# Two cross-attention layers: the beginning in a written order on all engines, loads queued behind the stacks, and a scale moved to ScalarE

## The chip, the cores and the metric

The kernel runs on one core of a Trainium2 chip. A core has a matrix engine (TensorE, PE in the profile), three engines for elementwise work (VectorE or DVE, ScalarE or ACT, GpSimd or POOL), a queue that does nothing here but issue transfers (SyncE or SP), and DMA engines that carry the transfers between the chip's memory and the on-chip buffers. Each engine works through its own list of instructions in order and waits on semaphores for the others. The metric is the device time of one launch in microseconds. Timed runs vary by a few us, and the profile is one more execution of the same program with the hardware profiler on.

## The reference: two attention layers with image tokens

The inputs are x (16 batches, 256 tokens, 320 channels) and a context of 16 x 256 tokens x 512 channels. Two layers follow one another, each with 20 heads of 16 channels. Cut to what matters, layer 0 is:

```python
text, ip = context[:, :77], context[:, 77:]          # 77 text tokens, 179 image tokens
q, k_text, v_text = x @ Wq, text @ Wk, text @ Wv
text_out = softmax(heads(q) @ heads(k_text).T / 4) @ heads(v_text)
scores = heads(q) @ heads(ip @ Wk_ip).T / 4
text_probs = softmax(q @ k_text.T / 4)               # over all 320 channels, no heads
sem = (text_probs @ text) @ ip.T / 4                 # the semantic term
ip_probs = softmax(scores + 0.5 * sem) * spatial_mask
out = (text_out + ip_probs @ heads(ip @ Wv_ip)) @ Wout + bout + x
```

Layer 1 takes that output as its x, with 252 text and 4 image tokens, and a semantic term for each head from normalised vectors. The change touches layer 0 only, in its beginning and in its repeated part.

## The kernel before

**Numbers.** Products with weights and context are made in a reduced float format (fp32r). Each operand is split into a high part and a low part: `halves` (L148 to L153) copies the high part on ScalarE (L150) and subtracts it from the source on VectorE or GpSimd (L153). A product is then three matmuls: high by high, high by low, low by high (`prod`, L238; `prod_m`, L248 for the third m-tile).

**Slots.** In layer 0 the 20 heads go in five groups of four, so 16 batches make 80 slots, each of one batch and one group. Slots 80 to 159 are layer 1. A slot of layer 0 has these steps:

- `stacks0` loads the slot's K and Q "stacks" by SP: 48 rows of keys or queries from the DRAM tiles kd and qd, which hold them as hi, hi, lo, and 77 rows that carry the semantic term (qs<-tph on the Q side, ks<-M on the K side). Two more rows carry the maxima and two constant "fields" that say to which token each maximum belongs. There are four stacks in a ring, and they are loaded four slots ahead (`LEAD`).
- `score0` multiplies them (PE, tile S, L728), and VectorE takes the maxima of text and image scores (L729, L730).
- `maxima0` turns the maxima on PE (L736), copies them on ScalarE (L738) and writes them into the Q stack with four small DMAs, issued by ScalarE (L740), or by SP for the first two slots.
- `turned0` makes the transposed scores with the maxima already subtracted (PE, tile T, L752), takes the exponential on ScalarE (L755), and GpSimd multiplies it by rs, the exponential of the semantic term (L758).
- `attend0` and `settle0` multiply by the values and normalise (L785, L796 to L803).

**Tasks.** Everything that is done per batch or per pair of batches is a task with due times in slots: keys (`keys0`, a pair at a time, with the context load and its split), queries (`queries0`: the x load, its split into hq at L583 to L585, three products at L595 and L598, the qd writes), semantic scores (`semantic0`), tokens, values, closing. The call `fill(now)` runs each task's next piece when its time has come. The order on PE is therefore written by hand everywhere.

**The other engines.** After the beginning, the order on SP, ScalarE, VectorE and GpSimd is chosen when the program is built, by a scheduler that simulates time. Only where `queued` is called, an instruction is kept behind the last one that was marked by `anchor` on its engine. In `begin`, all engines follow the order in which the instructions are written, but what stands before `begin` in the file (the loads and splits of the first weights and the first context in `all_halves`, the memsets, the fields) is placed by the scheduler.

**The beginning.** `keys_first` makes the first pair's keys: three m-tiles of text keys, then three of image keys, each m-tile over four chunks of the context before the next. Then come the first batch's queries, its semantic scores, the second batch's queries, the stacks and the first scores; SP issues all of it in one queue. PSUM, the matrix engine's output memory, is used in banks: two for T, one for P, three for X, and S.

**semantic0.** Of each batch it makes two tiles of 128 queries by 77 text tokens: scores (L651), their sum (L653 on ScalarE, L654), the maximum (L657, L658), the exponential with its sum (L662), the reciprocal (L665) and the scale by it (L666, VectorE), and the transposition on PE (L670) with its copies (L672, L673).

**Semaphores of the DMAs.** In the built program, the DMAs of SP and ScalarE take eight completion semaphores in turn, and each waits until the one before it on the same semaphore has completed. So which DMA a small maxima load waits for depends on how many DMAs lie between.

Of the kernel before, what the change touches and what calls it, by code (L numbers as in the profile page):

```python
# [17 lines left out]
S = 256  # L18
H = 20
# [30 lines left out]
def xattn2(  # L50
# [31 lines left out]
    def dma(out, in_):  # L82
        nc.sync.dma_start(*(f(ap) if ap.dtype == FR else ap for ap in (out, in_)))  # L83
# [5 lines left out]

    def bank(tag="X"):  # L90
        return ps.tile([128, 512], F32, tag=tag, name=tag, bufs=BANKS[tag])
# [35 lines left out]
    nc.scalar.copy(ident_r, ident)  # L127
    tmask = const_tile([128, 7], "tmask")
    dma(tmask, tmask_d)
# [89 lines left out]

    def all_halves(jobs, rings):  # L220

        waiting = []
        for src, hi, lo, tag in jobs:
            while sum(w[3] == tag for w in waiting) == rings[tag]:
                halves(*waiting.pop(0)[:3])
            raw = buf(tag, [128, 512], bufs=rings[tag])
            raw = raw[:, : src.shape[1]] if len(src.shape) == 2 else raw.rearrange("p (k n) -> p k n", k=src.shape[1])
            dma(raw, src)
            waiting.append((hi, lo, raw, tag))
        for w in waiting:  # L230
            halves(*w[:3])
# [30 lines left out]
    def context(b, n, wait=0):  # L262
# [8 lines left out]
        yield from in_turn(parts, wait, "rawc raw" if b == 2 and n == 2 else "rawc", nc.gpsimd if wait and b != 2 else nc.vector)  # L271
        if n == 2:
# [3 lines left out]

    ct = [buf(t, [128, 2, 512], FR, bufs=2, name="ct") for t in ("cta", "cta", "ctb", "ctb")]
    ctx0 = [(cT_d[k * 128 : (k + 1) * 128, : 2 * S], ct[k][:, 0], ct[k][:, 1]) for k in range(4)]
# [6 lines left out]
    RINGS = {"P": SIZES["NP"], "raw": SIZES["RAW"], "rawc": 2}  # L285
    all_halves(
        [job for k in range(4) for job in (
            (*ctx0[k], ("rawc", "raw")[k // 2]), (rows(wk0_d, k), *rounded(wkt[:, k]), "P"))],
        RINGS,
    )  # L290
    x0 = buf("xq", [128, 3, S])
    dma(x0, xT_d[0].rearrange("(k p) t -> p k t", p=128))
    all_halves(
        [(rows(wq0_d, k), *rounded(wqt[:, k]), ("rawc", "raw")[k // 2]) for k in range(3)]
        + [(rows(wki0_d, k), *rounded(w), "P") for k, w in enumerate(wkit)],
        RINGS,
    )
    nc.vector.tensor_scalar_mul(wqt[:, 2, CH : 2 * CH], f(wqt[:, 2, CH : 2 * CH]), tmask[:, 3:4])
    wvt, wvit = buf("wC", [128, 2, 4, 320], FR), [buf("wD", [128, 2, 2, 320], FR, bufs=2) for j in range(2)]
    all_halves(  # L300
        [(rows(wv0_d, k), wvt[:, 0, k], wvt[:, 1, k], ("rawc", "raw")[k % 2]) for k in range(4)]
        + [(rows(wvi0_d, k), wvit[k // 2][:, 0, k % 2], wvit[k // 2][:, 1, k % 2], ("rawc", "raw")[k % 2]) for k in range(4)],
        RINGS,
    )
    wv0, wvi0 = [lambda s, k: wvt[:, s, k]], [lambda s, k: wvit[k // 2][:, s, k % 2]]
    wq, wo = [lambda s, k, m: wqt[:, k, columns(s, m)]], []

# [3 lines left out]
    ind0 = buf("raw", [128, 512], bufs=SIZES["RAW"], name="ind0")[:2, :S]  # L311
    dma(ind0, ind0_d)
    ind0r = buf("mt", [8, S], FR, name="ind0r")[:2]
    nc.scalar.copy(ind0r, ind0)
    for i in range(SIZES["NR"]):
        nc.gpsimd.memset(f(ks[i]), 0.0)
        nc.gpsimd.memset(f(qs[i]), 0.0)
        dma(ks[i][XROW + T0 : KS0], ind0r.unsqueeze(1).to_broadcast([2, 4, S]))
# [3 lines left out]
    for v in vr:  # L322
        nc.gpsimd.memset(v, 0.0)
        for t in range(2):
            nc.vector.tensor_scalar_add(
                vcols(v, V0W)[:, t, :, 16], vcols(v, V0W)[:, t, :, 16], tmask[:, t : t + 1]
            )
        nc.vector.memset(vcols(v, V0W)[:, 2, :, 16], 1.0)
# [3 lines left out]
    nc.vector.memset(zone, 0.0)  # L332
    nc.vector.memset(zone[:, 21:22], 1.0)
    hsn = const_tile([128, 3, 8, 2, 16], "hsn")
    nc.gpsimd.memset(f(buf("q", [128, 2, 3, S], FR))[64:, :, 2], 0.0)
# [37 lines left out]
    def keys_first():  # L373
# [6 lines left out]
        for w, lo, hi, a, z in ((wk0, 0, T0 + 1, 0, T0), (wki0, T0 - 1, S, T0, S)):  # L380
            for m in range(3):
                kp = bank()[:, : 2 * (hi - lo)].rearrange("p (b t) -> p b t", b=2)
                prod_m(kp, w, m, lambda s, k: ct(s, k)[:, :, lo:hi], 4)
                n = 64 if m == 2 else 128
                evacuate(kst[m][:, 0, :, a:z], kst[m][:, 1, :, a:z], kp[:, :, a - lo : z - lo], m)
                if a:
                    keys_out(kd[0][0], m, kst[m], slice(0, 1))
                else:
                    nc.gpsimd.tensor_copy(kt[:n, m, :, :, :T0], f(kst[m][:n, :, :, :T0]))
                yield  # L390
# [188 lines left out]
    def split(src, neg, eng, tag):  # L579

        hl = buf(tag, [128, 5, S], FR)
        order = queued if tag == "hq" else lambda inst: inst
        order(nc.scalar.copy(hl[:, 0:3], src))  # L583
# [711 lines left out]
```

## Time and profile before

| | |
|---|---|
| median of 3 timed runs | 1550.69 us (1549.12 to 1552.69) |
| the profiled execution | 1542.26 us |
| its span | 1540.4 us |
| PE busy | 1441.0 us, 94% |
| VectorE busy | 1207.8 us, 78% |
| GpSimd busy | 1203.6 us, 78% |
| ScalarE busy | 872.8 us, 57% |
| mean granted clock of TensorE | 0.978 |
| HBM read, written | 118.04 MB, 77.10 MB |

The span is what the profile covers; the profiled execution's own time lies 1.86 us above it, and 8.43 us below the median of the timed runs. In rows of the timeline stand the start (us from the span's start), the duration, the engine, the line of the kernel, the operation, the tile written and the tiles read, and in brackets how long the engine was idle before and which engine, tile or line ended that. An engine name with a q (SPq, ACTq) is its sequencer, which issues DMAs. In the views of waits stand the engine and line that waited, what released it, the total in us, the count and the longest. In a table by windows stand, for each stretch, the busy time and count of each engine, TensorE's granted clock as a share of full speed, the DMA engines' busy share and GB/s. A PE row's end is modelled, and matmuls overlap, so PE's share says where it is idle better than how fast it works.

### The profile page before, as it was taken

To read this page: it belongs to the slowest core of one execution; us is meant where nothing else is said; L and a number is where in the kernel's file an instruction comes from. 1 tells how busy PE (TensorE), PEld (TensorE's weight loads), DVE (VectorE), ACT (ScalarE), POOL (GpSimd) and SP (SyncE) were. 2 spreads that over 40 slices of the span, in tenths; PEclk is the share of its full clock that TensorE was granted. 3 is DMA by queue.
4 is the path that set the end of the run, shared out by engine and by line. 5 is a ranking of instruction groups with operands and counts; after the bars stand their busy time and mean duration, and the time that the engine had idled before them with its cause. 6 is when DMAs were issued, how large, how long until landed. Compare 5 with 4: busy or idle time off the path is not lost.

```text
span 1540.4 us, 36105 instructions
## 1 busy us (share of the span) xinstructions
PE 1441.0 (94%) x12726; PEld 1162.6 (75%) x12726; DVE 1207.8 (78%) x2659; ACT 872.8 (57%) x1941; POOL 1203.6 (78%) x1274
## 2 busy tenths in 40 slices
PE   6789999999999989788999999999999999999996
PEld 5678888878787878567777777777777777777764
DVE  6458888777777788867778888888887887788885
ACT  5345555555564545546665666566656666666561
POOL 4258797979797978878587788877987798779785
PEclk9889999999999999989999999999999999999997
DMA  6756777676766666765444344444444344434311
GB/s 208 204 179 175 218 192 215 189 218 188 217 192 201 190 202 172 207 199 153 117 123 117 115 137 110 117 130 120 117 119 136 108 121 124 132 106 113 100 32 36
DMA packets 228815, 233.04 MB, mean 151 GB/s; under 512 B 38410, under 2 KB 198508, under 8 KB 228620
## 3 DMA queue, kind: packets, MB, share of 16 engines
q1 hardware_dynamic: 226428, 229.44, 52.5%
q8 instruction: 102, 1.67, 0.5%
q10 hardware_dynamic: 2208, 1.30, 0.3%
q14 instruction: 77, 0.63, 0.1%
HBM read 118.04 MB, written 77.10 MB: 127 GB/s over the span
## 4 chain that ended last, share of the span: by engine, by line
PE 57%; POOL 12%; DVE 11%; DMA 7%; issue 4%; ACT 3%; SPq 2%; ACTq 1%; DVEq 0%; POOLq 0%
PE X L238 12%; PE X L923 11%; POOL wt L914 5%; PE P L785 5%; PE X L595 5%; PE S L728 4%; PE P L935 3%; PE T L752 3%; PE P L945 3%; PE T L875 2%; PE S L881 2%; POOL P L758 2%; DMA qs<-qd 2%; SPq L83 2%; DVE wt L924 2%
## 5 line engine op out<-in xcount | busy, mean ns | idle before, releaser
L758 POOL TENSOR_TENSOR P<-P,rs 128x512 f32<-128x512 f32 x320 | 413.9, 1316 | 121.0 <-ACT P L755 120.5
L914 POOL TENSOR_TENSOR wt<-P,ctb 128x512 f32<-128x512 f32 x320 | 410.4, 1306 | 86.8 <-ACT ctb L913 85.8
L923 PE MATMUL X<-ctb,gm 128*128 128x512 f32 x1120 | 305.9, 402 | 6.4 <-DVE wt L924 6.3
L755 ACT ACTIVATE P<-T 128x512 f32<-128x512 f32 x320 | 176.3, 594 | 172.7 <-PE T L752 104.4
L924 DVE TENSOR_TENSOR wt<-X,wt 128x512 f32<-128x512 f32 x320 | 216.6, 681 | 46.9 <-PE X L923 41.2
L923 PEld LDWEIGHTS X<-ctb,gm 128*128 128x128 f32 x1120 | 195.7, 189 | 39.8 <-DVE wt L924 9.2
L895 ACT ACTIVATE P<-T 128x512 f32<-128x512 f32 x320 | 173.3, 594 | 76.5 <-PE T L875 74.2
L913 ACT ACTIVATE ctb<-P 128x512 fp32r<-128x512 f32 x320 | 187.0, 627 | 44.1 <-PE X L923 33.1
L883 DVE TENSOR_REDUCE mn<-S 128x4 fp32r<-128x1008 f32 x160 | 191.2, 1195 | 0.0
L730 DVE TENSOR_REDUCE mn<-S 128x4 fp32r<-128x716 f32 x160 | 142.3, 889 | 0.0
L785 PE MATMUL P<-P,vr 128*32 128x256 f32 x1920 | 127.7, 397 | 3.6 <-DVE mx L665 1.2
L728 PE MATMUL S<-ks,qs 125*128 125x256 f32 x640 | 117.5, 307 | 7.5 <-DMA qs<-tph 4.1
L728 PEld LDWEIGHTS S<-ks,qs 125*128 125x128 f32 x640 | 89.0, 196 | 43.1 <-issue 36.2
L752 PE MATMUL T<-qs,ks 127*128 127x256 f32 x640 | 108.4, 290 | 11.9 <-DVE tmp L802 6.4
L1011 POOL TENSOR_TENSOR r<-u,rs 128x40 f32<-128x40 f32 (+2 forms) x17 | 108.7, 6395 | 3.9 <-DVE u L1008 3.8
L752 PEld LDWEIGHTS T<-qs,ks 127*128 127x128 f32 x640 | 90.9, 194 | 14.9 <-DVE tmp L802 6.9
L729 DVE TENSOR_REDUCE mn<-S 128x4 fp32r<-128x308 f32 x160 | 74.2, 464 | 32.4 <-PE S L728 31.6
L796 DVE STREAM_TRANSPOSE nt<-P 128x512 f32<-128x512 f32 x80 | 56.9, 711 | 48.6 <-PE P L785 48.1
L785 PEld LDWEIGHTS P<-P,vr 128*32 128x32 f32 x1920 | 57.4, 112 | 45.6 <-issue 7.0
L595 PE MATMUL X<-hq,wE 128*128 128x256 f32 x512 | 79.2, 294 | 10.6 <-ACT hq L583 5.0
L935 PE MATMUL P<-P,v1t 128*32 128x256 f32 x1280 | 86.4, 388 | 0.2 <-DVE wt L924 0.2
L945 PE MATMUL P<-wt,zone 128*32 128x256 f32 x1280 | 85.1, 379 | 0.3 <-DVE wt L924 0.3
(235 smaller groups left out, 3004.9 us busy)
## 6 DMA issues: line engine op xcount, KB each, us to landing
qd<-q SPq DMA_DIRECT2D x96, 256.0 KB
qs<-tph SPq DMA_DIRECT2D x64, 308.0 KB
rawc<-in_cT_dram SPq DMA_DIRECT2D x60, 256.0 KB
qs<-qd SPq DMA_DIRECT2D x80, 192.0 KB
ks<-kd SPq DMA_DIRECT2D x80, 192.0 KB
ks<-kd SPq DMA_DIRECT2D x160, 96.0 KB
qs<-qd SPq DMA_DIRECT2D x160, 96.0 KB
kd<-kst SPq DMA_DIRECT2D x57, 256.0 KB
```

What stands on the lines that cost most here:

```text
L238: last = mm(out, lhs(a, k), rhs(b, k), start=i == 0, stop=i == len(terms) - 1)
L728: mm(sp[:, h], Q[: XROW + T0, h, t * 128 : (t + 1) * 128], K[: XROW + T0, h], start=True, stop=True)
L752: mm(st[p][:, j], K[:KS0, 2 * p + j, t * 128 : (t + 1) * 128], Q[:KS0, 2 * p + j], start=True, stop=True)
L755: exp = anchor(nc.scalar.activation(pt, st[p], AF.Exp, scale=SCALE))
L758: anchor(nc.gpsimd.tensor_mul(pt, pt, rs[:, t : t + 1].to_broadcast([128, 2, S])))
L785: mm(pv[32 * s : 32 * s + 32, o : o + S], v[:, vt, h : h + 32], P[k, s // 2][:, t, s % 2], start=vt < 2, stop=vt != 1,)
L883: anchor(nc.vector.tensor_reduce(maxes[k + 2][:, t], sp[:, :, :T1], axis=AX.X, op=ALU.max))
L895: anchor(nc.scalar.activation(P[k, u][:, t], st[u], AF.Exp, scale=SCALE))
L913: nc.scalar.activation(R[k, u][:, t], P[k, u][:, t], AF.Copy, scale=0.5)
L914: anchor(nc.gpsimd.tensor_sub(W[k, u][:, t], P[k, u][:, t], f(R[k, u][:, t])))
L923: mm(yp, gm[:, gb], R[k, u][:, kt], start=i == 0, stop=i == len(blocks[n]) - 1)
L924: nc.vector.tensor_mul(W[k, u][:, n], yp, W[k, u][:, n])
```

## The change

Three parts.

1. **The beginning.** The first loads and splits move from before `begin` into it, so that all engines follow a written order. `all_halves` goes; `land` issues loads and `cast` splits what has landed. The first context and key weights are loaded chunk by chunk, and x, tmask, the query weights, the image-key weights and the value weights after them. The text keys of `keys_first` are made chunk by chunk for all three m-tiles at once, in three banks. A list `turns` lends the banks of T and P to products that otherwise use X. The Q stacks' memsets are left out, those of the values are smaller, and they, the marks in the values and the memsets of the K stacks are on GpSimd. The fields are loaded by `fields` in the written order. The first batch's semantic scores are finished ahead of the second batch's query products, the second batch's tokens are made earlier, and the first stack's loads, the maxima of slot 0 and the values come in another order.
2. **The loads.** For every pair of batches after the second (b over 2), the context loads are kept behind the K stack load that was written last (`later`), and so are the x loads of the odd batches after the first (`late`); the x load of an odd batch is due at -5.4 slots instead of -4.4.
3. **The scale.** The 32 scales by the reciprocal in `semantic0` are done on ScalarE (an activation Copy with a scale) instead of VectorE.

```diff
@@ in_turn
-    def in_turn(parts, wait, tag="raw", eng=nc.vector):
+    def in_turn(parts, wait, tag="raw", eng=nc.vector, later=False):
...
-                dma(raw, src)
+                (queued if later else lambda inst: inst)(dma(raw, src))
@@ context
-        yield from in_turn(parts, wait, "rawc raw" if b == 2 and n == 2 else "rawc", nc.gpsimd if wait and b != 2 else nc.vector)
+        yield from in_turn(parts, wait, "rawc raw" if b == 2 and n == 2 else "rawc", nc.gpsimd if wait and b != 2 else nc.vector, n == 2 and b > 2)
@@ keys_first
-        for w, lo, hi, a, z in ((wk0, 0, T0 + 1, 0, T0), (wki0, T0 - 1, S, T0, S)):
+        out = lambda lo, hi: bank()[:, : 2 * (hi - lo)].rearrange("p (b t) -> p b t", b=2)
+        kp = [out(0, T0 + 1) for m in range(3)]
+        for k in range(4):
             for m in range(3):
-                kp = bank()[:, : 2 * (hi - lo)].rearrange("p (b t) -> p b t", b=2)
-                prod_m(kp, w, m, lambda s, k: ct(s, k)[:, :, lo:hi], 4)
...
+                terms = ((0, 0), (0, 1), (1, 0))[: 3 if m < 2 else 2]
+                for i, (a, c) in enumerate(terms):
+                    mm(kp[m], wk0(a, k, m), ct(c, k)[:, :, : T0 + 1], start=k + i == 0, stop=k == 3 and i == len(terms) - 1)
+            yield
@@ load, queries0
-        dma(x, src.rearrange("(k p) t -> p k t", p=128))
+        order = queued if late else lambda inst: inst
+        order(dma(x, src.rearrange("(k p) t -> p k t", p=128)))
...
-        x = x0 if b == 0 else load(xT_d[b], "xq")
+        x = b and load(xT_d[b], "xq", b > 1 and b % 2)
@@ semantic0
             nc.vector.reciprocal(zs, zs)
-            nc.vector.tensor_scalar_mul(tp, tp, zs)
+            nc.scalar.activation(tp, tp, AF.Copy, scale=zs)
@@ stacks0
-                dma(K[0:XROW], stack_rows(kd[0][b // 2][:, :, b % 2], g))
+                anchor(dma(K[0:XROW], stack_rows(kd[0][b // 2][:, :, b % 2], g)))
@@ tasks
-        task(("q0", 2 * c + 1), shifted(n, -4.4, -4, -3, -2.8, -2), lambda b=2 * c + 1: queries0(b))
+        task(("q0", 2 * c + 1), shifted(n, -5.4, -4, -3, -2.8, -2), lambda b=2 * c + 1: queries0(b))
@@ begin
+        def land(*names):
+            for n in names:
+                src, hi, lo, tag = first[n]
+                raw = landed[n] = buf(tag, [128, 512], bufs=SIZES["NP"] if tag == "P" else 2)[:, : src.shape[1]]
+                dma(raw, src)
+
+        def cast(*names):
+            for n in names:
+                halves(*first[n][1:3], landed[n])
+
+        named = lambda a: [(a, k) for k in range(4)]
+        for k in range(4):
+            land(("c", k), ("k", k))
+        dma(x0, xT_d[0].rearrange("(k p) t -> p k t", p=128))
+        dma(tmask, tmask_d)
+        constants()
+        for k in range(4):
+            turns.extend(["X"] * (3 if k == 0 else 0))
+            cast(("c", k), ("k", k))
+            parts(k0)
+            if k < 3:
+                land(("q", k))
+        nc.scalar.copy(ident_r, ident)
+        land(*named("i"))
+        xs0.append(split(x0, tmask[:, 5:6], nc.vector, "hq"))
+        for k in range(3):
+            cast(("q", k))
...
+        land(("v", 0), ("v", 1), ("v", 2))
+        fields()
+        marks()
+        turns.extend(["T", "T", "P", "X", "X", "X", "T"])
+        get(*m0)
+        parts(k0)
+        parts(q0, q0, q0, q0)
+        stacks0(0, "M")
+        parts(q0)
         get(*q0)
-        get(*m0)
-        parts(s0, s0, s0, s0, s0)
-        stacks0(0, "M")
+        cast(("i", 0), ("i", 1))
+        get(*m1)
+        parts(s0)
+        cast(("i", 2))
+        parts(s0)
+        cast(("i", 3))
+        parts(s0, s0, s0)
         stacks0(1, "M")
-        parts(k0, k0, k0, s0, q1, q1, q1, q1)
+        parts(q1)
+        turns.extend(["X", "T", "X", "X"])
+        parts(k0)
+        parts(s0)
+        cast(("v", 0), ("v", 1), ("v", 2))
+        land(("v", 3), *named("w"))
+        parts(k0)
+        cast(("v", 3))
+        parts(k0)
+        stacks0(0, "T")
         stacks0(0, "QK")
+        parts(q1)
+        cast(*named("w"))
         get(*s0)
-        stacks0(0, "T")
-        stacks0(1, "QKT")
-        get("v0", 0)
-        v1 = ("v0", 1)
+        parts(v0, q1, q1)
+        stacks0(1, "TQK")
+        parts(v0)
+        score0(0, 0)
+        parts(q1)
+        get(*q1)
+        parts(v0, k0)
+        get(*v0)
         stacks0(2)
-        parts(k0)
-        score0(0, 0)
-        parts(v1)
         score0(0, 1)
-        get("m0t", 1)
         maxima0(0, nc.sync)
-        parts(v1)
+        parts(v1, v1)
         get(*v1)
-        get(*q1)
         score0(1, 0)
         stacks0(3)
         score0(1, 1)
```

More of the change, by code (lines that the diff above doesn't have):

```diff
@@ L274, in context, with split @@
         return lambda s, k: tiles[k // 2][:, s, (k % 2) * S : (k % 2 + 1) * S]
+    def split(src, neg, eng, tag):
+        hl = buf(tag, [128, 5, S], FR)
+        order = queued if tag == "hq" else lambda inst: inst
+        order(nc.scalar.copy(hl[:, 0:3], src))
+        order(eng.tensor_sub(hl[:, 3:5], src[:, 0:2], f(hl[:, 0:2])))
+        order(nc.vector.scalar_tensor_tensor(hl[:, 2], f(hl[:, 2]), neg, src[:, 2], op0=ALU.mult, op1=ALU.add))
+        return hl
     ct = [buf(t, [128, 2, 512], FR, bufs=2, name="ct") for t in ("cta", "cta", "ctb", "ctb")]
-    ctx0 = [(cT_d[k * 128 : (k + 1) * 128, : 2 * S], ct[k][:, 0], ct[k][:, 1]) for k in range(4)]
     ct0 = {0: lambda s, k, tiles=ct: tiles[k][:, s].rearrange("p (b t) -> p b t", b=2)}
@@ L284, in xattn2 @@
     wki0 = lambda s, k, m: wkit[k][:, columns(s, m)]
[L285 to L290, printed above, removed]
-    x0 = buf("xq", [128, 3, S])
[L292 to L297, printed above, removed]
@@ L577, in tokens1 @@
         return V, G
[L579 to L583, printed above, removed]
-        order(eng.tensor_sub(hl[:, 3:5], src[:, 0:2], f(hl[:, 0:2])))
-        order(nc.vector.scalar_tensor_tensor(hl[:, 2], f(hl[:, 2]), neg, src[:, 2], op0=ALU.mult, op1=ALU.add))
-        return hl
     def project(l, w, a, evac):
```

98 lines of the change are left out of this document (49 added, 49 removed).

## The prediction

> **What bounds the kernel now.** I read the busy times and the 40 slices first, then tables by stage, then what TensorE (PE) waits for, and last the chain and the timeline where those waits lie. The page:
>
> ```profile
> PE 1441.0 (94%) x12726; PEld 1162.6 (75%) x12726; DVE 1207.8 (78%) x2659; ACT 872.8 (57%) x1941; POOL 1203.6 (78%) x1274
> ```
>
> PE is busy 94% of the span, and the change leaves its matmuls the same in number and shape; so what order can win is the 6% in which PE is idle, and the time in which its clock is low. The tables by stage say where those are:
>
> ```profile
> 0.00:70.00 70.00, 48.07 (x280) 44.80 (x281) 37.22 (x113) 30.65 (x76) 21.44 (x32) 0.94 0.72 211
> 301.00:378.00 77.00, 73.48 (x698) 63.21 (x698) 60.62 (x140) 43.33 (x102) 65.10 (x63) 1.00 0.71 205
> ```
>
> The columns are length, busy PE, weight loads, VectorE (DVE), ScalarE (ACT), GpSimd (POOL), PE's clock, DMA. The first 70 us hold 21.9 us of idle PE, a period of ten slots in layer 0 some 3.5, and layer 1 isn't touched. So the beginning is the large term, and the two others share about 3.5 us a period, with some seven periods.
>
> What PE waits for in the first 70 us (us in total, times, longest), then over the run:
>
> ```profile
> PE X L238 <- ACT wA L150: 6.5, 3, 5.1
> PE X L595 <- ACT hq L583: 5.0, 2, 3.0
> PE S L728 <- DMA qs<-tph: 4.1, 1, 4.1
> ```
> ```profile
> PE X L736 <- DVE mn L730: 8.8, 9, 2.5
> PE X L670 <- DVE sp L666: 4.3, 4, 2.6
> PE T L752 <- DMA qs<-mt: 3.0, 5, 1.0
> PE X L736 <- ACT P L755: 3.0, 2, 1.5
> ```
>
> **The change, part 1: the beginning.** The timeline of before, up to slot 0's exponential:
>
> ```profile
> 9.28 0.45 ACT L150 CAST wA<-P 128x320 fp32r<-128x320 f32 x1
> 10.45 0.43 SPq L83 DMA_DIRECT2D xq<-in_xT_dram  x1
> 14.24 1.06 PE L248 MATMUL X<-ctb,wA 128*128 128x156 f32 x4
> 23.40 1.27 PE L598 MATMUL X<-hq,wE 128*128 128x256 f32 x5
> 39.18 3.21 SPq L83 DMA_DIRECT2D qd<-q  x5
> 43.72 0.95 SPq L83 DMA_DIRECT2D qs<-tph  x1
> 49.11 1.19 PE L728 MATMUL S<-ks,qs 125*128 125x256 f32 x4 [4.07 <-DMA qs<-tph]
> 50.16 4.01 SPq L83 DMA_DIRECT2D kd<-kst  x4
> 54.21 1.28 SPq L83 DMA_DIRECT2D kd<-ho  x2
> 55.60 2.57 SPq L740 DMA_DIRECT2D qs<-mt  x4
> 62.79 1.08 ACT L755 ACTIVATE P<-T 128x512 f32<-128x512 f32 x2 [0.16 <-PE T L752]
> ```
>
> Text keys: the last weight chunk is cast at 9.73. Before, the first m-tile alone follows the chunks and the other two come after them, to 15.3. After, all three m-tiles take a chunk as it lands, and behind the last cast stand 8 matmuls, 2 us at the 0.25 of the 10-us rows (1.06/4): end about 11.5. Queries: x's load was issued at 10.45, behind some of the query weights; now it stands right behind the eight first loads, six us earlier, and the 20 matmuls end about 18.5 (24.7 before). The semantic scores and the image-token keys then follow to about 30, with one wait for the softmax inside them, taken at 1.5, the longest that the waits above show for an exponential (P).
>
> The SP queue decides next. Before, the first stack's loads stood behind the second batch's query writes (39.18), the last of them at 43.72; now those writes come later, and after 18.5 SP holds 3.2 of first query writes, the fields, then the key writes as the products end at 30. That puts the first stack's last load at about 34.8 and the first scores at 38 (49.1). Slot 0 needs the four small maxima loads, and they now stand behind stack 1 (three loads at 0.56 to 0.95 as in the rows here, 2.2), six key writes (4.0+1.3), five query writes (3.2) and stack 2 (four loads, 3.0): 34.8+13.7 = 48.5, with 2.6 for themselves 51.1. They land about 2.7 later (the row 310.45 below), so slot 0 starts at 53.8: **−9 us**. By waits: wA 6.5 down to 3, hq 5.0 to nothing, tph 4.1 to 2, a new 1.5: −9.1. It is no more, since SP's 13.7 us of issues take the place of PE's waits; beside them PE has the values and the second batch's queries to do, as long as the casts of the value weights are ahead of it. Bounds: −4 (only the text keys' 3.8 us are kept, and SP's queue eats the rest), −13 (the 11 us of the first scores in full, and 2 of clock).
>
> The clock in that stretch (columns as above):
>
> ```profile
> 44.00:48.00 4.00, 1.03 (x8) 0.77 (x6) 0.00 (x0) 0.44 (x1) 0.00 (x0) 1.00 0.89 226
> 48.00:52.00 4.00, 2.89 (x12) 2.92 (x13) 1.29 (x2) 0.00 (x0) 0.00 (x0) 0.57 0.87 198
> 64.00:80.00 16.00, 12.39 (x67) 9.64 (x68) 10.84 (x17) 6.05 (x14) 8.59 (x8) 0.57 0.53 137
> ```
>
> PE was busy 1.03 of 4 us, and then the granted clock was 0.57: of 2.89 busy us 1.2 were lost to it. After, no wait before slot 0 comes near 4 us, so I count that 1.2 as won (it is inside the −9). The second cold stretch, 0.57 from 64 to 80, lies behind slot 0, where the queues of the beginning are still being worked off; I leave it in the forecast, and its going is rival b. The Trainium skill ("TensorE: Matmul & The Clock Gate", Why this matters for your kernels) says that idle gaps over about 3 us between bursts of matmuls bring PE back to half clock. The rows from 44 to 52 agree; by that rule alone the second stretch would go too, and the sum would be 5.3 lower (rival b), if the gaps ahead of it shrink below 3 us.
>
> **Part 2: the loads.** In a period of layer 0, x for the odd batch (xq) and the next pair's context (rawc) were loaded 46 and 57 us before their casts, as the rows below show. The chain, then the timeline of all engines (in brackets the idle time before, and what ended it):
>
> ```profile
> 304.78 5.64 DMA qs<-qd
> 310.45 2.66 DMA qs<-mt
> ```
> ```profile
> 306.27 1.01 SPq L83 DMA_DIRECT2D rawc<-in_cT_dram  x2
> 308.59 2.42 ACTq L740 DMA_DIRECT2D qs<-mt  x2
> 309.75 0.38 SPq L83 DMA_DIRECT2D xq<-in_xT_dram  x1
> 311.12 1.09 ACT L755 ACTIVATE P<-T 128x512 f32<-128x512 f32 x2 [2.94 <-DMA qs<-qd]
> 348.90 0.56 SPq L83 DMA_DIRECT2D ks<-kd  x1
> 354.76 0.31 SPq L83 DMA_DIRECT2D ks<-kd  x1
> 355.56 0.84 ACT L583 CAST hq<-xq 128x768 fp32r<-128x768 f32 x1
> 363.79 1.15 ACT L150 CAST cta<-rawc 128x512 fp32r<-128x512 f32 x2
> ```
>
> A maxima load issued by ACT took 2.42 us to go out: in the program it waits for an earlier load of the same completion semaphore, a stack load that took 5.64 us with rawc and xq beside it, and ACT stood 2.94 us and PE 1.53. After, rawc and xq are queued behind the K stack loads about 48 us later and the semaphores rotate, so that this maxima load waits for an older one. The waits that name it are 3.0 (P) and 3.0 (qs<-mt) over the run: **−6 us**, one for each of the six contexts that move. Bounds: 0, if the next late thing (the maxima mn, 8.8 us in 9 waits) takes the gap; −10, with half of those 8.8, which come in the slots behind. Cost on the other side: SP issues the two rawc loads (1.01) and xq (0.38) ahead of a Q stack load, which is needed slots later (LEAD is 4), so nothing; and the loads have 8.7 us (rawc, issue at about 355, cast 363.79) and 6.1 (xq, about 349.5 to 355.56), against a landing of 3.3 at the start (issued at 0.74):
>
> ```profile
> 0.74 0.41 SPq L83 DMA_DIRECT2D rawc<-in_cT_dram  x1
> 4.06 0.62 ACT L150 CAST cta<-rawc 128x512 fp32r<-128x512 f32 x1 [2.04 <-DMA rawc<-in_cT_dram]
> ```
>
> **Part 3: the scale.** 32 instructions move from DVE to ACT; ACT's nearest row is a copy of the same tile:
>
> ```profile
> L653 ACT COPY sp<-X x32: 223/226/255, 27.3 to 628.3; 128x77 f32<-128x77 f32 x32
> L666 DVE TENSOR_SCALAR sp<-sp,mx x32: 264/890/1274, 29.0 to 635.2; 128x77 f32<-128x77 f32 x32
> 225.77 0.21 ACT L662 ACTIVATION_READ_ACCUMULATOR sp<-sp,mx 128x1 f32 x1
> 229.14 0.15 DVE L665 RECIPROCAL mx<-mx 128x1 f32<-128x1 f32 x1
> ```
>
> DVE loses 32×0.89 = 28.5 us, ACT (57% busy) gains about 32×0.25 = 8. On the path only the 4.3 us in which PE waited for sp, taken as **−3**; with a little of the mn waits, which also end on DVE, −5. Against it, ACT works in order, and the scale waits for DVE's reciprocal: at 229.14 that came 3.2 us after the sum, with exponentials behind. One such wait is hidden where ACT waits for PE anyway; bound +3.
>
> **Sum.** −9 −6 −3 = −18 from this execution's 1542.26, which is 8.4 below the median of the runs shown: 1524.3, or **1533** against 1550.69. The lower ends add up to −28, the upper to −1.
>
> **Rivals.** (a) Forecast: 0.60.
> (b) The second cold stretch goes too, as PE has work ordered closer behind slot 0. The time lost from 64 to 80 is busy time by 1 less the clock, 12.39×0.43 = 5.3, so 1527. For: the first stretch followed a gap. Against: the first slots still need DVE, POOL and SP one after the other, and those rows show PE idle 3.6 of 16 us. 0.10.
> (c) The beginning alone pays, and the other two only change what PE waits for (mn): −9, 1542. For: mn is the largest wait. 0.14, of which 0.03 within 0.2%.
> (d) Slower: ACT waits in order for reciprocals behind a busy DVE, and the exponentials and maxima loads stand behind it. At 3.2 us in each of 16 batches 51 at the most; with the other parts' 15 won it decides from 15 on. If PE pays 22, 1550.69+7 = 1558. For: the 3.2 at 229.14. Against: PE's order keeps a slot of scores between, and 15 of the 51 must reach it. 0.09, of which 0.02 within 0.2%. The Trainium skill ("Perfetto Trace Analysis", Tensor Engine Instruction) says ACT and DVE are strict FIFO, which is this rival's mechanism; 308.59, where the exponentials stood behind a maxima load, agrees.
> (e) Slower: context lands late. Each us late is paid in six contexts: 4 us late is +24, less 9+3 won +12: 1563; it decides from 2 us on. Against: 8.7 us stand for 3.3. 0.07, of which slower 0.04, same 0.02, faster 0.01.
> Faster 0.82, within 0.2% (±3.1 us, about what a measurement of this kernel can tell) 0.07, slower 0.11. The range goes from 1517 (all lower ends and b: −28−5.3) to 1550 (all upper ends), with 0.17 outside, nearly all of it d, e and no change.
>
> **What would show it.** Slot 0's exponential at 53 to 55, first scores at about 38 after no idle over 3 us, full clock at 48; no ACT stand over 2 us at the maxima loads of each period, and about 1 us less idle PE than 3.5 in a period of 77; no PE wait for sp. Wrong if SP's queue ends the beginning at 60 or later, if ACT rows show idle before the scale with L755 behind, or if the rawc or xq casts wait for DMA.

## The result, and the profile after

The changed kernel took 1531.87 us (median of four runs, 1526.83 to 1538.38) against 1551.69 us for the kernel before (1549.12 to 1552.9), a ratio of 0.9881 with a 95% interval of 0.9854 to 0.9908: 1.2% faster. The forecast was 1533. Line numbers of the changed kernel differ from those of before: L755 is now L749, L728 is L722, L752 is L746, L736 is L730, L670 is L664, L666 is L660, L740 is L734, L595 is L588, L598 is L591, L238 is L226; L150 and L153 are L151 and L154, and L380 makes the first text keys.

The profiled execution after took 1531.06 us. From its page:

```profile
span 1529.3 us, 36083 instructions
PE 1440.8 (94%) x12726; PEld 1163.5 (76%) x12726; DVE 1183.0 (77%) x2618; ACT 881.5 (58%) x1973; POOL 1195.6 (78%) x1279
```

PE's busy time is that of before (1441.0). VectorE lost 24.8 us of work, ScalarE gained 8.7, as the 32 scales went over. The tables by windows of after, columns as in the prediction:

```profile
0.00:70.00 70.00, 51.09 (x291) 46.73 (x291) 37.33 (x104) 33.45 (x85) 17.93 (x39) 0.89 0.75 222
301.00:378.00 77.00, 75.44 (x713) 65.32 (x713) 60.14 (x142) 45.03 (x108) 67.16 (x65) 1.00 0.72 208
```

PE is busy 3.0 us more of the first 70, and 2.0 more of the same 77 us of layer 0, whose idle time fell from 3.5 to 1.6. What PE waited for, first in the first 70 us and then over the run:

```profile
PE X L380 <- ACT wA L151: 5.2, 2, 5.1
PE X L226 <- ACT wC L151: 2.7, 1, 2.7
PE S L722 <- DMA ks<-M: 1.2, 1, 1.2
```
```profile
PE X L730 <- DVE mn L724: 7.0, 8, 2.2
PE X L664 <- ACT sp L660: 6.1, 3, 3.9
PE T L746 <- DMA qs<-mt: 2.4, 5, 0.9
```

In the beginning the wait for tph is gone, those for hq fell from 7.1 us (on three engines) to 1.9, and one for the value weights (wC) is new. Of the 5.2 us for wA, 5.1 stand at the very start, as before. Over the run the wait of L736 for P (3.0) is gone, and that for the scaled probabilities sp, which part 3 was to shorten, is longer (6.1 for 4.3).

The span is only 11.1 us shorter than that of before, where the medians differ by 19.8. Both kernels were profiled a second time below, and that pair differs by 18.4 us in span (1542.6 and 1524.2). One execution of scale_alone below, at 2693.43 us, is left out of its ratio.

### The profile page after: what moved, and what is told of

The parts are those of the page before. It is cut to its first block, busy times and chain, and to the rows that moved or that the text cites. A ratio compares the mean times of both kernels' runs of the same rounds, so it can differ in the third digit from the quotient of the medians.

```text
span 1529.3 us, 36083 instructions
## 1 busy us (share of the span) xinstructions
PE 1440.8 (94%) x12726; PEld 1163.5 (76%) x12726; DVE 1183.0 (77%) x2618; ACT 881.5 (58%) x1973; POOL 1195.6 (78%) x1279
## 3 DMA queue, kind: packets, MB, share of 16 engines
q8 instruction: 102, 1.67, 0.5%
## 4 chain that ended last, share of the span: by engine, by line
PE 33%; POOL 8%; DVE 6%; issue 2%; ACT 2%; DMA 1%; ACTq 1%; DVEq 0%; SPq 0%; POOLq 0%
PE X L917 11%; PE X L226 5%; POOL wt L908 5%; PE P L929 3%; PE X L588 3%; PE P L939 3%; PE T L869 2%; PE S L875 2%; DVE wt L918 2%; PE X L1042 1%; POOL hq L270 1%; POOL r L1005 1%; DVE mn L877 1%; PE X L236 1%; DVE ho L271 1%
## 5 line engine op out<-in xcount | busy, mean ns | idle before, releaser
L752 POOL TENSOR_TENSOR P<-P,rs 128x512 f32<-128x512 f32 x320 | 414.3, 1316 | 113.5 <-ACT P L749 112.2
L749 ACT ACTIVATE P<-T 128x512 f32<-128x512 f32 x320 | 176.0, 594 | 157.1 <-PE T L746 92.9
L722 PE MATMUL S<-ks,qs 125*128 125x256 f32 x640 | 116.0, 304 | 4.5 <-DVE mn L724 1.3
L746 PE MATMUL T<-qs,ks 127*128 127x256 f32 x640 | 109.8, 293 | 9.4 <-DMA qs<-mt 2.4
L722 PEld LDWEIGHTS S<-ks,qs 125*128 125x128 f32 x640 | 87.7, 193 | 39.6 <-issue 33.4
L746 PEld LDWEIGHTS T<-qs,ks 127*128 127x128 f32 x640 | 91.8, 196 | 12.9 <-ACT P L749 2.7
L779 PEld LDWEIGHTS P<-P,vr 128*32 128x32 f32 x1920 | 57.4, 113 | 44.6 <-issue 7.9
L588 PE MATMUL X<-hq,wE 128*128 128x256 f32 x496 | 77.2, 295 | 7.1 <-POOL hq L270 3.2
```

The source lines that it names most:

```text
L722: mm(sp[:, h], Q[: XROW + T0, h, t * 128 : (t + 1) * 128], K[: XROW + T0, h], start=True, stop=True)
L746: mm(st[p][:, j], K[:KS0, 2 * p + j, t * 128 : (t + 1) * 128], Q[:KS0, 2 * p + j], start=True, stop=True)
L749: exp = anchor(nc.scalar.activation(pt, st[p], AF.Exp, scale=SCALE))
L752: anchor(nc.gpsimd.tensor_mul(pt, pt, rs[:, t : t + 1].to_broadcast([128, 2, S])))
L779: mm(pv[32 * s : 32 * s + 32, o : o + S], v[:, vt, h : h + 32], P[k, s // 2][:, t, s % 2], start=vt < 2, stop=vt != 1,)
```

## The experiments

Slots are read from the first exponential of each (L755, L749): the table at the end of this section gives for each profile when slot 0 and slot 10 start, and how long slots 10 to 50 take, that is four of the periods of ten slots.

**The parts one by one.** Each part alone on the kernel before, and the changed kernel without its third part.

```diff
# begin_alone: changed kernel
-        yield from in_turn(..., n == 2 and b > 2)
+        yield from in_turn(...)
-        x = b and load(xT_d[b], "xq", b > 1 and b % 2)
+        x = b and load(xT_d[b], "xq", False)
-        shifted(n, -5.4, -4, -3, -2.8, -2)
+        shifted(n, -4.4, -4, -3, -2.8, -2)
-                anchor(dma(K[0:XROW], stack_rows(kd[0][b // 2][:, :, b % 2], g)))
+                dma(K[0:XROW], stack_rows(kd[0][b // 2][:, :, b % 2], g))
-            nc.scalar.activation(tp, tp, AF.Copy, scale=zs)
+            nc.vector.tensor_scalar_mul(tp, tp, zs)
# loads_alone: kernel before, with the late loads of the changed kernel
# scale_alone: kernel before, with the scale of the changed kernel
# all_but_scale: changed kernel
-            nc.scalar.activation(tp, tp, AF.Copy, scale=zs)
+            nc.vector.tensor_scalar_mul(tp, tp, zs)
```

> The beginning of the changed kernel alone; context and x loads unqueued and the scale on VectorE, as before. By the forecast: -9 us (ratio 0.994), slot 0 near 54 and the lead kept to slot 10. By the two traces: slot 0 at 58.6 for 62.8 and slot 10 at 157.6 for 159.6, so only -2 to -4 (0.997 to 0.999), as half of the lead at slot 0 is gone by slot 10. Rival: the beginning changes where the semaphores of the DMAs fall in every later slot, and takes the 2.4 us stall of the maxima loads away by itself: then slots 10 to 50 are faster too, and the ratio is 0.993 or less.

> The kernel before with the context loads and odd x loads queued behind the K stack loads, nothing else. By the forecast: -6 us (0.996). By the two traces: slots 10 to 50 took 301.8 for 309.3, -7.5 us (0.995), slot 0 unchanged at 62.8. Rival: that the gain of those slots comes from the scale or from where the semaphores fall: then slots 10 to 50 stay at 309 and the ratio is 0.999 to 1.001.

> The kernel before with the 32 scales on ScalarE, nothing else. By the forecast: -3 us (0.998), PE waits for sp near 1. By the two traces, where PE waits for sp rose from 4.3 to 6.1 us: +2 (1.001), with the waits now named for ScalarE. Rival d of the forecast, ScalarE held in order by VectorE's reciprocals: +7 or more (1.005).

> The changed kernel with the scale back on VectorE. By the forecast it is 3 us slower than the changed kernel, near 1535 (0.990 of before). If the scale costs, as the waits for sp in the trace after say, it is 1 to 3 us faster than the changed kernel, near 1530 (0.986). If the scale does nothing, 0.988.

Measured, each as ratio to the kernel before on the same chip (median 1549.02): the beginning 0.9925 (0.9895 to 0.9954), the loads 0.9965 (0.9946 to 0.9985), the scale 0.9979 (0.9957 to 1.0002), everything but the scale 0.9882 (0.9845 to 0.9919). So the beginning and the loads gain, each by itself, which rules out rival c of the forecast, and the scale adds nothing that shows beside them: the kernel without it has the changed kernel's ratio. By medians the three parts alone are −12.4, −4.3 and −2.7 us, together −19.4, nearly the −19.8 of the whole. In scale_alone PE's waits for sp are 6.2 us, where the forecast put 1. In the profiles, the beginning alone starts slot 10 at 154.4 (159.6 before) and leaves slots 10 to 50 at 312.2 (309.3); the loads alone take those 40 slots to 305.6. That refutes the rival by which the beginning took the stall out of the later slots, though the ratio that it named (0.993 or less) came about.

**Both kernels again, and the changed kernel without the loads.**

```diff
# all_but_loads: changed kernel
-        yield from in_turn(..., n == 2 and b > 2)
+        yield from in_turn(...)
-        x = b and load(xT_d[b], "xq", b > 1 and b % 2)
+        x = b and load(xT_d[b], "xq", False)
-        shifted(n, -5.4, -4, -3, -2.8, -2)
+        shifted(n, -4.4, -4, -3, -2.8, -2)
-                anchor(dma(K[0:XROW], stack_rows(kd[0][b // 2][:, :, b % 2], g)))
+                dma(K[0:XROW], stack_rows(kd[0][b // 2][:, :, b % 2], g))
```

> The kernel before once more, for a second profile. Its first profiled execution took 1542.26 us, the others 1543 to 1558. If single executions differ by chance collisions of a few us each (a VectorE instruction of 0.5 to 0.8 us that takes 3 to 6 us beside GpSimd, as at 134.80 in the trace with the loads alone), slots without one have the same length to 0.1 us in both profiles and the rest sits in a few slots. Rival: the whole of layer 0 or layer 1 is slower by a constant share in the longer executions; then most slots are longer by 0.5%.

> The changed kernel once more, for a second profile and more times. By the sum of the parts alone (-12.4, -4.3, -2.7 by medians) a ratio near 0.9875; by the first two profiles alone (-11.1) near 0.993. Slots 10 to 50 take 302 us again, slot 0 starts at 58.6.

> The changed kernel with context loads and odd x loads unqueued as before: beginning and scale. By the forecast 6 us slower than the changed kernel (0.992). By the mechanism (a maxima load that waits for a slow stack load of its semaphore), slot 9 of each period takes 9 us again, for 6.5 in the changed kernel, with the stall on ScalarE's DMA issue. Rival: with the scale on ScalarE the DMA order is another anyway and slot 9 stays below 7.5; then the ratio is that of the changed kernel, 0.988.

The changed kernel again: 0.9863 (0.9828 to 0.9899), 1527.47 us beside 1547.61. Without the loads: 0.9975 (0.9950 to 1.0000), 1544.89 us. That is the surprise. With the scale on VectorE and the loads early (begin_alone) the ratio was 0.9925; the same with the scale on ScalarE is slower, by 0.5%, with intervals that just touch. In the profiles, PE's wait for sp, first with the scale on VectorE (begin_alone), then on ScalarE (all_but_loads):

```profile
PE X L664 <- DVE sp L660: 3.6, 2, 2.9
```
```profile
PE X L664 <- ACT sp L660: 6.9, 4, 3.5
```

So what moving the scale is worth seems to hang on the loads. In slots 10 to 50, by profile:

| | scale on VectorE | scale on ScalarE |
|---|---|---|
| context early | 309.3, 312.6, 312.2 (mean 311.4) | 313.9, 315.7, 318.1 (mean 315.9) |
| context and x late | 305.6, 305.4, 309.8 (mean 306.9) | 301.8, 302.4, 303.9, 303.3 (mean 302.9) |

In these profiles the scale costs 4.5 us with the context early and gains 4.0 with it late; the loads gain 4.5 with the scale on VectorE and 13.0 with it on ScalarE. The cells hold three or four profiles each, and two of the first cell are executions of the kernel before that lie 3 to 9 us under the medians measured with them. By the timed runs the cost shows in one pair only, begin_alone and all_but_loads; on the kernel before, the scale alone was not slower (0.9979).

Slot by slot, the scale on ScalarE lengthens the ninth slot of each period and shortens the tenth, wherever the loads stand: over the four periods by +4.1 and −3.1 us with the context early, by +3.0 and −5.5 with it late. Over the run, PE's waits for the maxima loads (qs<-mt at L752 or L746) rise with it from 4.5 to 6.3 us on average with the context early, and from 1.9 to 2.4 with it late.

The second profile of the kernel before also shows how its executions can differ. Most slots (129 of 159) have the length of the first profile to 0.1 us, so the rival of a constant share falls. The three largest differences, 1.6 to 3.0 us, are in slots 10, 40 and 50, each the first of a period, where PE's clock dropped in one of the two profiles. The table by windows of the kernel before, in its first profile and in its second:

```profile
158.00:162.00 4.00, 4.00 (x46) 3.16 (x47) 2.90 (x9) 1.67 (x4) 3.38 (x4) 1.00 0.80 249
162.00:166.00 4.00, 4.00 (x31) 4.00 (x31) 3.10 (x7) 1.64 (x4) 3.36 (x4) 1.00 0.78 217
```
```profile
158.00:162.00 4.00, 3.28 (x15) 3.11 (x15) 1.97 (x6) 1.45 (x3) 3.05 (x4) 0.55 0.84 274
162.00:166.00 4.00, 4.00 (x33) 2.14 (x33) 1.51 (x4) 0.29 (x1) 1.66 (x3) 0.60 0.43 136
```

The same program, at the same place: once at full clock, once at half for most of 8 us. That slot (10) took 8.6 us in the one and 11.4 in the other. Worked out from such tables of 4 us (busy time by 1 less the clock), PE lost between 150 and 526 us 3.3 to 6.3 us to a low clock in each of the six profiles with the context early, and 0 to 3.2 us in the eight with it late (0.0 and 0.1 in the two of the changed kernel).

**Which load, and why.** The two kinds of loads were put back one at a time.

```diff
# x_late_only: changed kernel, context early
-        yield from in_turn(..., n == 2 and b > 2)
+        yield from in_turn(...)
# context_late_only: changed kernel, x early
-        x = b and load(xT_d[b], "xq", b > 1 and b % 2)
+        x = b and load(xT_d[b], "xq", False)
-        shifted(n, -5.4, -4, -3, -2.8, -2)
+        shifted(n, -4.4, -4, -3, -2.8, -2)
```

> The changed kernel with the context loads early again; only the odd x loads are late. In the program, slot 30's last maxima load then again waits for a Q stack load just issued (qs<-qd), and slot 31's first for a context load. By the theory of the semaphores: the 2 to 3 us stall on ScalarE's DMA issue is back, the tenth slot of each period takes 9 us. By the theory of shared DMA bandwidth (0.38 MB of the 0.9 MB moved away): between, near 8.

> The changed kernel with the odd x loads early again and due at -4.4 slots; only the context loads are late. In the program, the maxima loads of slots 30 and 31 then wait for older loads (ks<-M, small loads) or for none. By the theory of the semaphores: tenth slots take 6.5 to 7 us, the whole gain, ratio to before near 0.987. By that of shared bandwidth: some 7.5, as xq still goes out beside them.

With only x late: 0.9996 (0.9970 to 1.0021); with only the context late: 0.9913 (0.9885 to 0.9942), beside 1547.32. The tenth slots of the four periods took 9.0, 9.3, 7.7 and 9.3 us (mean 8.8) with x late, 7.1, 7.0, 8.0 and 7.8 (7.5) with the context late, and 6.3 to 6.7 (6.5) with both (9.5 before). In all_but_loads, which has the scale on ScalarE as these two have, and neither load late, they took 8.7. So the context is most of it; x late gains nothing by itself, and 1 us beside the late context. The theory of the semaphores put 9 and 6.5 to 7, that of shared bandwidth 8 and 7.5: each has one of the two right. With only the context late, PE's chain from 296 to 318 us holds no DMA, so the stall itself is gone there; that xq's share of the bandwidth makes the last 1 us is argued from the 7.5, not seen. The chain of waits with only x late shows the stall as it stood before, a slow Q stack load and behind it the maxima load that waits for it:

```profile
303.62 5.46 DMA qs<-qd
309.10 3.48 DMA qs<-mt
```

and the table by windows of the same profile, what came of it:

```profile
306.00:310.00 4.00, 3.72 (x42) 2.87 (x35) 2.68 (x7) 1.38 (x5) 2.49 (x3) 1.00 0.97 306
310.00:314.00 4.00, 2.47 (x14) 1.93 (x13) 2.35 (x6) 1.89 (x6) 2.90 (x3) 0.89 0.82 281
314.00:318.00 4.00, 4.00 (x32) 2.40 (x31) 0.67 (x2) 1.23 (x3) 2.89 (x3) 0.50 0.47 138
318.00:322.00 4.00, 4.00 (x24) 3.72 (x21) 2.77 (x6) 1.09 (x2) 1.30 (x2) 0.76 0.16 49
```

PE was idle 1.5 of the 4 us from 310 to 314, and the next 6 us or so went at half clock, which lost 2.47×0.11+4.00×0.50+4.00×0.24 = 3.2 us: the stall costs twice. In the changed kernel the maxima loads of that place go out without a stall. The last two of the slot's four start 0.63 us apart (304.07 and 304.70), where 1.59 us lie between them with only x late (307.51 and 309.10). The timeline of the changed kernel:

```profile
301.30 0.57 ACTq L734 DMA_DIRECT2D qs<-mt  x1
302.49 0.57 ACTq L734 DMA_DIRECT2D qs<-mt  x1
304.07 0.57 ACTq L734 DMA_DIRECT2D qs<-mt  x1
304.70 0.57 ACTq L734 DMA_DIRECT2D qs<-mt  x1
343.85 0.44 SPq L83 DMA_DIRECT2D xq<-in_xT_dram  x1
350.44 0.96 SPq L83 DMA_DIRECT2D rawc<-in_cT_dram  x2
350.81 0.84 ACT L269 CAST hq<-xq 128x768 fp32r<-128x768 f32 x1
358.75 1.15 ACT L151 CAST cta<-rawc 128x512 fp32r<-128x512 f32 x2
```

The late loads have 7.0 us (xq) and 8.3 us (rawc) before their casts, and neither cast waits for its DMA.

**The beginning, with its own new wait taken out.** The timeline of the changed kernel up to slot 0:

```profile
9.23 3.98 PE L380 MATMUL X<-ctb,wA 128*128 128x156 f32 x16 [0.17 <-ACT wA L151]
17.81 0.75 PE L591 MATMUL X<-hq,wE 128*128 128x256 f32 x5
28.57 0.47 SPq L83 DMA_DIRECT2D raw<-in_wv_dram  x1
33.48 1.33 PE L226 MATMUL X<-wC,ctb 128*128 128x320 f32 x3 [2.68 <-ACT wC L151]
37.31 3.57 PE L588 MATMUL X<-hq,wE 128*128 128x256 f32 x15 [1.07 <-POOL hq L270]
42.57 0.64 PE L722 MATMUL S<-ks,qs 125*128 125x256 f32 x4
46.08 2.17 SPq L83 DMA_DIRECT2D kd<-kst  x4
53.48 2.79 SPq L734 DMA_DIRECT2D qs<-mt  x4
57.44 0.71 PE L722 MATMUL S<-ks,qs 125*128 125x256 f32 x4 [1.18 <-DMA ks<-M]
58.61 1.09 ACT L749 ACTIVATE P<-T 128x512 f32<-128x512 f32 x2 [0.26 <-PE T L746]
```

The last chunk of the value weights is issued at 28.57, PE waits 2.68 us for it at 33.48, and the second batch's queries behind it run at half clock:

```profile
36.00:40.00 4.00, 2.93 (x13) 2.69 (x13) 3.20 (x6) 1.84 (x5) 1.26 (x1) 0.50 0.62 173
48.00:52.00 4.00, 4.00 (x29) 4.00 (x29) 0.00 (x0) 1.10 (x3) 0.00 (x0) 1.00 0.75 219
64.00:80.00 16.00, 12.28 (x79) 9.29 (x77) 9.99 (x15) 6.72 (x14) 8.85 (x9) 0.76 0.55 152
```

The next kernels load that chunk with the other three, and move six key writes on SP behind slot 1's maxima.

```diff
# weights_early_keys_late: changed kernel
-        land(("v", 0), ("v", 1), ("v", 2))
+        land(("v", 0), ("v", 1), ("v", 2), ("v", 3))
-        land(("v", 3), *named("w"))
+        land(*named("w"))
-        parts(v0, k0)
+        parts(v0)
         maxima0(1, nc.sync)
+        parts(k0)
# early_keys_vector_scale: the same, and
-            nc.scalar.activation(tp, tp, AF.Copy, scale=zs)
+            nc.vector.tensor_scalar_mul(tp, tp, zs)
# early_keys_vector_context: as weights_early_keys_late, and in context
-        nc.gpsimd if wait and b != 2 else nc.vector
+        nc.gpsimd if wait and b not in (2, 4) else nc.vector
```

> The changed kernel with the last chunk of the first value weights loaded with the other three, and the second batch's six key writes moved on SP from ahead of stack 2 to behind slot 1's maxima. In the trace after, PE waited 2.7 us for that chunk and SP had 4.3 us of key writes ahead of stack 2, which the scores ahead of slot 0's exponential need. By the theory that SP's queue sets slot 0: slot 0 near 54 (58.6), -4 us, and part of it kept to slot 10. Rival: slot 0 comes sooner but slots 1 to 5 take longer, as PE's work of the beginning only moves behind it; then slot 10 stays at 157 to 158 and the time is that of the changed kernel.

> As weights_early_keys_late (last value chunk loaded early, six key writes behind slot 1's maxima), with the scale on VectorE: the candidate to beat both kernels. In that run slot 0 came at 53.7, and 5.6 us were lost again in slot 7, where a VectorE subtraction that started 0.04 us behind a GpSimd one took 5.91 us for 1.66. If that is a matter of where the two happen to meet, this order may miss it: then slot 10 near 150 and 1523 to 1526 us. If it meets it again: 1530 to 1534.

> As weights_early_keys_late, with one more edit: the low parts of the third pair's context (the one that is split in slot 7) are subtracted on VectorE instead of GpSimd, so that the GpSimd instruction beside which the VectorE subtraction took 5.91 us isn't there. By the theory of the collision: slot 7 takes 7 to 9 us for 12.9, and the kernel is 4 to 5 us faster than weights_early_keys_late, near 1529. Rival, that VectorE's long subtraction had another cause (a late input): slot 7 stays near 13 and the time is the same or longer, by 4 x 0.7 us more work on VectorE.

Ratios: 0.9901 (0.9867 to 0.9935), 0.9903 (0.9876 to 0.9931) and 0.9913 (0.9884 to 0.9942). None beats the changed kernel; early_keys_vector_scale took 1528.68 us, where 1523 to 1526 were expected. Slot 0 came at 53.7, 54.2 and 53.7, 2 to 5 us sooner; slot 10 came at 155.0, 151.5 and 153.7, where the two profiles of the changed kernel have 157.6 and 152.3. Only a part of the gain at slot 0 is SP's queue: at 57.44 above, PE waited 1.18 us for stack 2's last load (0.48 in the second profile), and in weights_early_keys_late the same row, at 52.66, has no wait. The rest was won earlier on PE: the first scores came at 38.87 us for 42.57 and 41.38, as the wait for the chunk was gone and the second batch's 15 query matmuls took 2.04 us for 3.57. The two edits were not run apart. Nor do these kernels show whether a sooner slot 0 is kept: in the first of them slot 7 took 12.9 us (7.3 in the changed kernel), by this VectorE row:

```profile
126.34 1.29 POOL L154 TENSOR_TENSOR cta<-rawc,cta 128x512 fp32r<-128x512 f32 x1
126.38 5.91 DVE L270 TENSOR_TENSOR ho<-hT,ho 128x512 fp32r<-128x512 f32 x1 [1.35 <-ACT ho L269]
```

With the context's subtraction on VectorE (early_keys_vector_context) that row took 0.68:

```profile
126.03 2.84 DVE L154 TENSOR_TENSOR cta<-rawc,cta 128x512 fp32r<-128x512 f32 x2
128.79 0.68 DVE L270 TENSOR_TENSOR ho<-hT,ho 128x512 fp32r<-128x512 f32 x1
```

Slot 7 fell to 8.9 us, as the theory of the collision has it, yet the kernel was not 4 us faster (1532.23 for 1533.66): slot 8 took 1.5 us more, slot 1 0.6 and layer 1 some 2, and whether that is more than chance was not tried. The variant with the scale on VectorE missed the collision by itself (slot 7: 7.4) and lost elsewhere (slots 10 to 50: 309.8, for 305.4 in all_but_scale).

| profile | slot 0 | slot 10 | slots 10 to 50 | us of the execution |
|---|---|---|---|---|
| before | 62.8 | 159.6 | 309.3 | 1542.26 |
| before_again | 63.3 | 160.1 | 312.6 | 1544.42 |
| begin_alone | 57.7 | 154.4 | 312.2 | 1539.31 |
| loads_alone | 63.3 | 163.6 | 305.6 | 1545.06 |
| scale_alone | 63.1 | 161.0 | 313.9 | 1546.40 |
| all_but_scale | 57.1 | 153.5 | 305.4 | 1535.83 |
| all_but_loads | 56.9 | 160.4 | 315.7 | 1547.19 |
| x_late_only | 57.1 | 154.4 | 318.1 | 1545.03 |
| context_late_only | 58.0 | 155.0 | 307.0 | 1533.43 |
| after | 58.6 | 157.6 | 301.8 | 1531.06 |
| changed_again | 56.6 | 152.3 | 302.4 | 1526.00 |
| weights_early_keys_late | 53.7 | 155.0 | 303.9 | 1533.03 |
| early_keys_vector_scale | 54.2 | 151.5 | 309.8 | 1532.38 |
| early_keys_vector_context | 53.7 | 153.7 | 303.3 | 1532.06 |

## Why the prediction was right, and which terms were not

The total held (1533 forecast, 1531.87 measured). The loads were right in mechanism, the beginning in its first steps, the scale not. Three sizes were off, and they cancelled: that the total came so near is in part luck.

*Beginning, −9.* Text keys: 13.2 for 11.5 (the forecast's own 9.73 and 2 us make 11.7). First queries: 18.6 (17.81+0.75), as forecast (18.5). The waits for wA, counted down to 3 us, stayed at 5.2, since 5.1 of them are the start of the kernel. The step that failed is the first scores at 38: they came at 42.6 and 41.4, since the last value chunk was late; with that chunk early they came at 38.9. The prediction had named that condition ("as long as the casts of the value weights are ahead of it") without pricing it. The SP sum from there had the right list of issues: the maxima loads went out at 53.48 for 48.5, and slot 0 came at 58.6 and 56.6 instead of 53.8. But SP's queue was not what mostly set slot 0. PE was behind by then, and waited for SP only 1.18 and 0.48 us. That slot 0 came at 53.7 with the late chunk and the key writes out of the way is no proof of the sum, which has those writes in it. By slot 10 the lead was −2.0 in the first pair of profiles, −7.8 in the second, and −5.2 for the beginning alone. Over the four profiles with the old beginning and the seven with the new one as it was changed, slot 0 starts at 63.1 and 57.4 us on average and slot 10 at 161.1 and 155.4: a lead of 5.7 us that is kept, under two thirds of the term. The timed ratio of the beginning alone is −7 to −16 us; the profiles account for less than its lower end, and the rest stays open.

*Clock (rival b).* The first cold stretch moved rather than went: 0.50 at 36 to 40 us for 0.57 at 48 to 52, so the 1.2 us counted as won there was not. The second is milder at its old place (0.76 for 0.57 from 64 to 80), but slot 0 is earlier, and 58 to 66 is cold instead (0.50 and 0.64). From 34 to 150 us PE lost 9.7 and 12.9 us to the clock in the two profiles of before, 12.3 and 13.0 in those of the changed kernel: rival b did not happen.

*Loads, −6.* The mechanism stood: place, waits and remedy were as forecast, the tenth slot went from 9.5 to 6.5 us, and the casts found their loads landed (rival e did not happen). One row was misread: the 2.42 us at 308.59 are two maxima loads of 0.57 each, and the second was held for the rest, 1.3 us, until the Q stack load had landed (304.78+5.64 = 310.42). And not all of the tenth slot's 3.0 us are the loads': with them late and the scale on VectorE it takes 7.7 (loads_alone) and 7.6 (all_but_scale), and what the scale takes off beyond that it adds in part to the ninth slot. Alone, the loads were right in size (−2 to −8 us by the timed ratio). The size was too small where they go with part 3: all_but_loads against the changed kernel is 0.9975 to 0.9863 and 0.9881, 15 to 17 us. Left out of the term was the half clock behind the stall, some 3 us each time that it strikes; the first profile of before showed none of it in the periods that were read.

*Scale, −3.* Alone, the scale measured the forecast's 3 us (0.9979), but not clear of nothing, and not by its mechanism. PE's waits for sp did not fall: 4.3 and 4.4 us in the two profiles of before, 6.2 with the scale alone, 6.1 and 2.6 after. What fell is the wait for the maxima mn, from 8.8 and 8.8 to 7.0 and 7.3 (10.9 in all_but_scale). Net, the changed kernel's ratio with and without it is the same within the intervals (0.9881 and 0.9863; 0.9882). And rival d, ScalarE held in order, is not a fancy: with the context early, the scale on ScalarE costs 4.5 us in 40 slots by the profiles, and some 0.5% of the run by the times of one pair (begin_alone and all_but_loads), though nothing by those of the kernel before. That it did not decide because the late loads take away the stalls that it adds to is argued from the interaction: the waits for qs<-mt point that way, but they grow by 1.8 and 0.5 us, where the slots differ by 8.5.

*The sum against one execution.* The −18 was taken from 1542.26 and shifted by 8.4 to the median. The two profiles of before (1542.26 and 1544.42) both lie under the medians of its runs (1547 to 1552). Drops of the clock (some 3 us each) and collisions of VectorE with GpSimd (some 5) come in some profiles and not in others; that they explain this difference was not seen, as no execution near 1550 was profiled.

## What to carry to other kernels

A short stall on the busiest engine is worth more than its waiting time where the clock falls behind it: price a stall of 1 to 1.5 us at that plus the half clock (some 3 us here), and look at several profiles, as the drop comes in one execution and not in the next. A big load that isn't needed yet does harm where small, urgent loads go out; move it beside work that has slack, and count which earlier DMA each urgent one waits for. Moving work to a less busy engine that works in order pays only when what it waits for comes on time: try it alone and with the other changes, since here its effect on the slots turned with them.

## What the runs showed of the hardware

The clock fell to 0.50 after a 4-us stretch in which PE was busy 2.47 us and no single wait was over 1.04 us (with only x late, 310 to 314 us). The Trainium skill ("TensorE: Matmul & The Clock Gate", Why this matters for your kernels) warns of idle gaps over about 3 us. These rows are stricter, as several short gaps in one stretch did it, and at 158 us of the kernel before it struck in one execution and not in the other.

The clock records of the fourteen traces say more. The clock changes only at steps of 3.41 us, and these steps lie elsewhere in each execution. Cut at them, the stall with only x late fell into one step, while a like stall of the kernel before, in its first profile, was split over two. The tables by windows, first with only x late, then before:

```profile
309.71:313.12 3.41, 1.88 (x13) 1.34 (x11) 1.98 (x6) 1.97 (x5) 2.67 (x3) 1.00 0.85 306
313.12:316.53 3.41, 3.41 (x25) 2.81 (x27) 0.91 (x3) 1.38 (x4) 2.24 (x3) 0.50 0.73 214
```
```profile
307.99:311.41 3.42, 2.25 (x18) 2.04 (x18) 2.91 (x7) 0.48 (x2) 1.73 (x2) 1.00 1.02 275
311.41:314.82 3.41, 2.75 (x22) 2.48 (x22) 2.33 (x6) 1.86 (x6) 2.96 (x3) 1.00 0.90 312
```

All 188 drops stand at the end of a step in which PE was busy 2.52 us or less. Some 200 other such steps had no drop behind them, so this share alone doesn't tell which will.

The VectorE subtraction of two tiles in slot 7 (ho) took 5.91 to 5.92 us in the three profiles in which it started 0.02 to 0.04 us behind a GpSimd subtraction, 0.68 in the one without that subtraction beside it, and 1.65 to 1.67 us in the other ten, where it started 0.18 to 0.19 us behind it, as in the kernel before:

```profile
133.47 1.30 POOL L153 TENSOR_TENSOR cta<-rawc,cta 128x512 fp32r<-128x512 f32 x1
133.65 1.66 DVE L584 TENSOR_TENSOR ho<-hT,ho 128x512 fp32r<-128x512 f32 x1 [1.36 <-ACT ho L583]
```

In the long case it ended only when GpSimd's next instructions were through as well, 0.55 us after the last of them. So starts 0.15 us apart go with times 4 us apart in these fourteen profiles; no run moved the start alone. The Trainium skill ("GPSIMD Engine Reference", Specifications) says that GpSimd shares its memory interfaces with VectorE, and that VectorE instructions with two inputs in that memory contend with it; the rows agree, and add how much a start just behind GpSimd's costs.
